# Two moves of TensorE work inside the sixteen steps of a selective scan: the sums over states, the first convolution and the time-step projection

## The chip, the cores and the metric

The kernel runs as one program on one core of one Trainium2 chip. The metric is the device time of one execution in microseconds (us). Everything is fp32. A measurement of this kernel tells changes of about 0.2% from none.

## What is computed

The program is four layers one after the other on x of shape (2, 128, 64, 64). The change touches layer 0 only, a four-way selective scan (Mamba): the 4096 tokens of each of the 2 images are normalised over the 128 channels and scanned in four directions (row by row and column by column, each forwards and backwards), and the four outputs go through one fusing projection and are added to x. One direction is, cut to what matters:

```python
xz = x @ W_in.T
xh, z = jnp.split(xz, 2, axis=-1)              # 256 inner channels each
xh = silu(causal_conv4(xh) + conv_b)
x_dbl = xh @ W_xp.T                            # 8 for dt, 16 for B, 16 for C
dt = softplus(x_dbl[..., :8] @ W_dt.T + b_dt)
dA  = exp(dt[..., None] * A)                   # A: 256 channels x 16 states
dBu = dt[..., None] * Bm[:, :, None, :] * xh[..., None]
h_t = dA_t * h_{t-1} + dBu_t                   # scan over tokens
y = einsum('lbdn,bln->bld', hs, Cm) + xh * Dp  # sum over the 16 states
out = (y * silu(z)) @ W_out.T
```

Layers 1 and 2 are attention over 4096 positions, layer 3 is a second, small Mamba with a group norm. They are the same before and after.

## The kernel before, in words

**Chunks and steps.** Layer 0 is cut into 64 chunks of T = 512 tokens: image, then row or column order, then forwards or backwards, then 8 chunks (`chunks`). Chunks 0-7, 16-23, 32-39 and 48-55 run forwards, the others backwards. A chunk has 16 steps (`for s in range(16)`), one per unit u of 128 x 1024 elements: 128 partitions hold 4 states x 32 channels, and the free axis holds 2 blocks of 512 tokens. The order of all instructions is written out by hand under `tc.manual_schedule()`; each engine works off its own instructions in that order. Three chunks are in flight: `c` is scanned, `new` (the next) has its time step and B, C prepared, `nxt` (the one after) has its convolution made. `old` is the chunk before.

**One step s**, in the order of the source:

- `s_dbu` (L330, POOL): dBu of unit s+2. `dbu` has three buffers, so it waits for the scan of unit s-1.
- `s_scan` (L374, DVE): the scan of unit s.
- `V[s]`: extra DVE work, `dt_` (L306) in steps 5 and 6, the norm's `mul` (L194) in step 8 and `sub` (L161) in step 13.
- `s_hc` (L386 on DVE, or L384 on POOL for units 0, 5, 9, 11, 14): h times C for unit s-1. `hc` has four buffers.
- `s_da` (L343, ACT): dA of unit s+1 into one of two PSUM buffers, so it waits for the scan of unit s-1; `s_fix` (L358, ACT): adds the carried state to the first token of dBu of unit s+1. The scan of unit s+1 waits for it. The first chunk of a direction has no `s_fix`.
- `s_hst` (L379, ACT), then the list `A[s]` of extra ACT work.
- on TensorE (PE): `y0` (L390) in steps 3 and 11, the sums over states `s_y` (L397), then `M[s]`, then `s_pc` (L363), which spreads C over the partitions for `s_hc` two units at a time.
- `yg_(1)` of the old chunk at the end of step 1 and `yg_(0)` at the end of step 10 (L404, DVE): y times the gate.

**The sums over states.** `s_y(u)` is two matmuls of 128*32 by 128x512; a pair of units is 4 matmuls, 8 passes in the records. `pairs` says in which step a pair is issued: units 0,1 in step 3; 2,3 in 5; 4,5 in 8; 6,7 in 9; 8,9 in 12; 10,11 in 14; 12,13 in 15; 14,15 in step 1 of the next chunk. Units 0-7 add into one `y` tile and 8-15 into the next; `y` has one buffer. So `yg_(0)` waits for the sum of units 6,7 and `yg_(1)` for that of 14,15.

**The tile `misc`.** All other PSUM results of layer 0 share one PSUM buffer, `misc`: each user is a matmul in `M[s]` and a reader on ACT or DVE, and the next matmul into `misc` waits for that reader. In order: step 15 `pd` (L267), step 0 reader `xd_` (L272); `pt(0)` (L287, the time step's projection), reader `abs_(0)` (L294) in step 1; `pt(1)` in step 1, readers `abs_(1)` and then `e_exp` (L297) in step 2; `po` (L415, L419) in step 2, reader `xo` in step 4; `pt` again in steps 4 and 5 for `dt_`; `pz(0)` (L241) in step 6 with reader `z_` (L247); the norm's `scale` (L191) in step 7; `px(0)`, the first convolution (L228, four matmuls, 8 passes), in step 8 with its reader `x_(0)` (L237) in step 9; `px(1)` in step 10 with `x_(1)` in step 12; the norm's `center` (L157) in step 12; `pz(1)` in step 13; the norm's `var` (L170) in step 14. `e_ln` (L300, with a table load ahead of it and one after it) is in step 3.

**Norms and turns.** The normalisation of later tokens is mixed into chunks 0-3 and 15-22, its second half (`lp`: `rows`, `scale`, `mul`, `affine` L197) into the chunk after each. Chunks 6-13 and 32-39 have one copy more on ACT in step 11, which turns the picture. Below, "norm chunks" are chunks 1-4 and 16-22, which hold a second half of a norm (and all but chunk 4 a first half too); "plain forward" chunks are the other forward ones that are not first in their direction, 18 in number; "backward" chunks that are not first number 28.

Of the kernel before, what the change touches and what calls it, by code (L numbers as in the profile page):

```python
# [56 lines left out]
def conv_seq_kernel(ctx: ExitStack, tc: tile.TileContext, a: dict, out: bass.AP):  # L57
# [36 lines left out]
    with ExitStack() as c0:  # L94
# [104 lines left out]
        def turn(j):  # L199

            nc.scalar.copy(
                xnt[:, 3 + j * T : 3 + (j + 1) * T].rearrange("p (w h) -> p w h", h=H),
                xn[:, 3 : L + 3].rearrange("p (h w) -> p w h", w=W)[:, 8 * j : 8 * j + 8, :],
            )
# [234 lines left out]
        pairs = {}  # L439
# [3 lines left out]
        with tc.manual_schedule():  # L443
            c, c1 = chunks[:2]
# [110 lines left out]
            old = None  # L555
            for k, c in enumerate(chunks):
                new, nxt = (chunks[k + i] if k + i < nk else None for i in (1, 2))
                ln, lp = norms.get(k), norms.get(k - 1)

                def at(u):  # L560
                    return (c, u) if 0 <= u < 16 else ((old, u + 16) if u < 0 else (new, u - 16))

                A, V, M, G = {}, {}, {}, {}
                if old is not None:
                    M[2], A[4] = old.po, (old.xo,)
                if c.rev:
                    A[4] = (*A[4], c.zload)
                else:  # L570
                    A[8] = (c.zsilu,)
                if new is not None:
                    A[0] = (new.xd_,)
                    M[0], A[1] = lambda: new.pt(0), (lambda: new.abs_(0),)
                    M[1], A[2] = lambda: new.pt(1), (lambda: new.abs_(1), new.e_exp)
                    A[3] = (new.e_ln,)
                    M[4], V[5] = lambda: new.pt(0), lambda: new.dt_(0)
                    M[5], V[6] = lambda: new.pt(1), lambda: new.dt_(1)
                    G[7], G[8] = lambda: new.dtu_(0), lambda: new.dtu_(1)
                    if not new.rev:  # L580
                        M[6], A[7] = lambda: new.pz(0), (lambda: new.z_(0),)
                        M[13], A[14] = lambda: new.pz(1), (lambda: new.z_(1),)
                if nxt is not None:
                    M[8], A[9] = lambda: nxt.px(0), (lambda: nxt.x_(0),)
                    M[10], A[12] = lambda: nxt.px(1), (lambda: nxt.x_(1),)
                    A[13] = (nxt.xsilu,)
                    M[15] = nxt.pd
                if lp is not None:
                    A[3] = (*A[3], lp.ln, lp.exp)
                    A[6] = (lp.rows,)  # L590
                    M[7], V[8] = lp.scale, lp.mul
                    A[10] = (lp.affine,)
                if ln is not None:
                    M[12], V[13] = ln.center, ln.sub
                    A[14] = (*A.get(14, ()), ln.square)
                    M[14], A[15] = ln.var, (ln.keep,)
                if k in turns:
                    A[11] = (lambda: turn(turns[k]),)

                for s in range(16):  # L600
                    (c1, u1), (c2, u2), (cp, up) = at(s + 1), at(s + 2), at(s - 1)

                    if c2 is not None:
                        c2.s_dbu(u2)
                    c.s_scan(s)
                    if s in V:
                        V[s]()
                    if cp is not None:
                        cp.s_hc(up)
                    if s in G:  # L610
                        G[s]()

                    if c1 is not None:
                        c1.s_da(u1)
                        c1.s_fix(u1)
                    if cp is not None:
                        cp.s_hst(up)
                    for f in A.get(s, ()):
                        f()

                    if s in (3, 11):
                        c.y0(s // 11)
                    for cy, e in ((c, s), (old, s + 16)):
                        for u in pairs.get(e, ()) if cy is not None else ():
                            cy.s_y(u)
                            cy.s_y(u + 1)
                    if s in M:
                        M[s]()
                    if s % 2 and s < 15:
                        c.s_pc(s + 1)  # L630
                    elif s == 15 and new is not None:
                        new.s_pc(0)

                    if s == 1 and old is not None:
                        old.yg_(1)
                    if s == 10:
                        c.yg_(0)

                    if new is not None:
                        if s in (7, 14):  # L640
                            new.spread("dts", s // 14)
                        if s in (9, 13):
                            new.spread("dus", s // 13)
                        if s in (8, 10, 12, 14):
                            new.states(0, s // 2 - 4)
                        if s in (11, 12, 13, 15):
                            new.states(1, GROUPS_C[{11: 0, 12: 1, 13: 2, 15: 3}[s]])
                old = c
# [20 lines left out]
    with ExitStack() as c1:  # L669
# [296 lines left out]
        for n, j in enumerate(jobs):  # L966
# [10 lines left out]
            if jobs[n - 1].layer == 1:  # L977
                for ci in range(NCH):
                    c = Conv(jobs[n - 1].b, ci)
# [3 lines left out]
        with tc.manual_schedule():  # L983
# [13 lines left out]
            for slot in range((len(groups) + 2) * UPG):  # L997
                u = slot % UPG
                G = at(slot)[0]
                if G is not None:  # L1000
                    G.score(u)
                    nxt = at(slot + UPG)[0]
                    if u == 10 and nxt is not None:
                        nxt.q = nxt.job.query(nxt.g)
                G, d = at(slot - 1)
                if G is not None:
                    G.larger(d)
                G = at(slot - UPG)[0]
# [7 lines left out]
                G, d = at(slot - UPG - 5)  # L1016
                if G is not None and d % 2 == 0:
                    G.prob(d // 2)
                G, d = at(slot - UPG - 6)
                if G is not None and d % 2 == 0:  # L1020
                    G.expo(d // 2)
                G, d = at(slot - UPG - 8)
                if G is not None:
                    G.value(d)
                G, d = at(slot - UPG - 7)
                if G is not None and d % 2 == 0 and d:
                    G.total(d // 2)
                G, d = at(slot - 2 * UPG)
# [13 lines left out]
    with ExitStack() as c3:  # L1042
# [269 lines left out]
        V, G = nc.vector, nc.gpsimd  # L1312
# [6 lines left out]
        with tc.manual_schedule():  # L1319
            c = chunks[0]  # L1320
# [13 lines left out]
            for s in range(-1, len(steps) + 3):  # L1334
# [3 lines left out]
                old = chunks[ci - 1] if ci > 0 else None  # L1338
# [209 lines left out]
```

## Time and profile before

| what | value |
|---|---|
| three runs | 6811.3, 6818.59, 6804.39 us; median 6811.3 |
| the profiled execution | 6810.44 us, span 6808.7 us (1.7 us outside the span) |
| granted TensorE clock, mean | 0.857 |
| layer 0, first scan to end of the last | 57.15 to 3474.5 us of the span: 3417.35 us |
| busy in that stretch | PE 2898.43, DVE 3271.78, ACT 2749.80, POOL 3271.53 us |
| layers 1-3 | 3474.5 to 6808.7 us |
| one norm chunk (chunk 18) | 1028.11 to 1084.86: 56.75 us; DVE 52.37, POOL 51.30, ACT 48.23 busy |
| one plain forward chunk (chunk 53) | 2897.67 to 2951.37: 53.70 us; DVE 51.31, POOL 51.59, ACT 45.76 |
| one backward chunk (chunk 30) | 1686.60 to 1739.70: 53.10 us; DVE 51.08, POOL 50.99, ACT 41.39 |

How to read it: a chunk starts where its first scan (L374) starts, so every sixteenth L374 record of the trace is a chunk's start, and the distance between two scans is the length of a step. A timeline line has the start in us from the span's start, the length in us, engine, line, operation, tiles and count; in brackets stands how long the engine sat idle just before and what it is taken to have waited for. Consecutive records of the same kind are merged in it, with their number after "x".

### The profile page before, as it was taken

To read this page: it belongs to the slowest core of one execution; us is meant where nothing else is said; L and a number is where in the kernel's file an instruction comes from. 1 tells how busy PE (TensorE), PEld (TensorE's weight loads), DVE (VectorE), ACT (ScalarE), POOL (GpSimd) and SP (SyncE) were. 2 spreads that over 40 slices of the span, in tenths; PEclk is the share of its full clock that TensorE was granted. 3 is DMA by queue.
4 is the path that set the end of the run, shared out by engine and by line. 5 is a ranking of instruction groups with operands and counts; after the bars stand their busy time and mean duration, and the time that the engine had idled before them with its cause. 6 is when DMAs were issued, how large, how long until landed. Compare 5 with 4: busy or idle time off the path is not lost. (4 is left out here: it accounts for less than half of the span.)

```text
span 6808.7 us, 67303 instructions
## 1 busy us (share of the span) xinstructions
PE 6005.6 (88%) x20652; PEld 2821.7 (41%) x20652; DVE 5524.3 (81%) x4499; ACT 4461.8 (66%) x7666; POOL 5362.4 (79%) x2487
## 2 busy tenths in 40 slices
PE   8888888888888888888879999999999997888888
PEld 2222222222222222222238887787788884222222
DVE  7999999999999999999966665565566675787777
ACT  7887778877788777887745664555456564434342
POOL 6899998899999999999956664555566666777776
PEclk7777777777778777777779999999999998988888
DMA  6565655566566656665630000000000001222221
GB/s 170 138 149 145 157 145 140 137 154 150 141 159 152 157 143 154 150 154 146 148 93 2 4 4 1 1 1 1 1 1 13 1 1 61 75 71 72 90 75 67
DMA packets 352652, 616.51 MB, mean 91 GB/s; under 512 B 72473, under 2 KB 74786, under 8 KB 351650
## 3 DMA queue, kind: packets, MB, share of 16 engines
q1 hardware_dynamic: 351552, 610.44, 35.2%
q8 instruction: 162, 2.65, 0.2%
q14 instruction: 200, 1.64, 0.1%
q10 hardware_dynamic: 738, 1.78, 0.1%
HBM read 496.45 MB, written 115.47 MB: 90 GB/s over the span
## 5 line engine op out<-in xcount | busy, mean ns | idle before, releaser
L330 POOL TENSOR_TENSOR dbu<-dus,bs 128x1024 f32<-128x1024 f32 x1024 | 2404.0, 2374 | 157.0 <-DVE h L374 141.1
L374 DVE TENSOR_TENSOR_SCAN h<-da,hst,dbu 128x1024 f32<-128x1024 f32 x896 | 2094.3, 2345 | 77.8 <-ACT dbu L358 75.0
L343 ACT ACTIVATE da<-dts,aneg 128x512 f32<-128x512 f32 (+1 forms) x2048 | 1412.6, 690 | 443.7 <-DVE h L374 404.1
L890 POOL TENSOR_TENSOR sum<-sum,sc 128x1024 f32<-128x1024 f32 x384 | 906.8, 2362 | 496.7 <-ACT sc L885 493.1
L852 ACT COPY sc<-s 128x512 f32<-128x512 f32 x1024 | 598.1, 585 | 867.7 <-PE s L847 753.5
L859 DVE TENSOR_TENSOR mx<-mx,s 128x512 f32<-128x512 f32 x896 | 610.1, 681 | 569.5 <-ACT sc L852 568.5
L847 PE MATMUL s<-q,k 128*128 128x256 f32 x4096 | 1058.0, 382 | 11.7 <-ACT q L833 8.4
L902 PE MATMUL av<-sc,v 128*128 128x256 f32 x4096 | 1049.6, 379 | 2.3 <-ACT sc L885 2.3
L397 PE MATMUL y<-hc,cst 128*32 128x512 f32 x4096 | 811.3, 760 | 179.2 <-DVE hc L386 103.8
L386 DVE TENSOR_TENSOR hc<-h,pc 128x1024 f32<-128x1024 f32 x704 | 844.9, 1200 | 0.1
L847 PEld LDWEIGHTS s<-q,k 128*128 128x128 f32 x4096 | 781.2, 192 | 146.2 <-issue 36.6
L902 PEld LDWEIGHTS av<-sc,v 128*128 128x128 f32 x4096 | 769.1, 190 | 103.1 <-ACT sc L885 3.7
L384 POOL TENSOR_TENSOR hc<-h,cs 128x1024 f32<-128x1024 f32 x320 | 758.2, 2369 | 1.3 <-issue 1.3
L363 PE MATMUL pc<-xd,sel 16*128 16x512 f32 x1024 | 713.4, 788 | 4.8 <-DVE hc L386 4.1
L1217 POOL TENSOR_TENSOR A<-A,D 128x1024 f32<-128x1024 f32 x224 | 525.9, 2365 | 225.2 <-DVE D L1222 200.3
L882 DVE TENSOR_TENSOR sc<-sc,pm 128x1024 f32<-128x1024 f32 x512 | 620.9, 1214 | 0.9 <-PE pm L878 0.9
L885 ACT ACTIVATE sc<-sc 128x1024 f32<-128x1024 f32 x512 | 542.3, 1059 | 8.6 <-DVE sc L882 8.1
L287 PE MATMUL misc<-xd,w_dt 9*128 9x512 f32 x504 | 386.5, 855 | 155.1 <-ACT x L426 83.6
L1210 ACT ACTIVATE A<-dtr,aneg 128x1024 f32<-128x1024 f32 (+1 forms) x256 | 246.0, 1032 | 380.8 <-PE y L1242 363.0
L397 PEld LDWEIGHTS y<-hc,cst 128*32 128x32 f32 x4096 | 104.9, 117 | 745.6 <-issue 337.4
L1228 DVE TENSOR_TENSOR A<-A,q 128x1024 f32<-128x1024 f32 (+1 forms) x256 | 276.9, 1082 | 148.4 <-PE q L1194 148.2
L1194 PE MATMUL q<-xs,lb 32*128 32x512 f32 x896 | 331.5, 712 | 72.0 <-DVE D L1204 65.7
(263 smaller groups left out, 8078.4 us busy)
## 6 DMA issues: line engine op xcount, KB each, us to landing
dts<-ddt SPq DMA_DIRECT2D x512, 256.0 KB, 5.5
dus<-ddu SPq DMA_DIRECT2D x512, 256.0 KB, 5.1
bs<-rows SPq DMA_DIRECT2D x1024, 64.0 KB, 4.9
cs<-rows SPq DMA_DIRECT2D x1024, 64.0 KB, 3.3
ddt<-dt SPq DMA_DIRECT2D x128, 256.0 KB, 2.0
ddu<-dtu SPq DMA_DIRECT2D x128, 256.0 KB, 4.1
dtr<-ddt SPq DMA_DIRECT2D x448, 64.0 KB, 1.9
rx<-ddx SPq DMA_DIRECT2D x448, 64.0 KB, 1.9
```

What stands on the lines that cost most here:

```text
L330: nc.gpsimd.tensor_mul(t, self.dus[q], _bc(self.bs[g], 1, [P, 2, T]))
L343: act(t[:, i, sl], self.dts[q][:, i, sl], AF.Exp, scale=an[:, g, 2 * q + i : 2 * q + i + 1])
L363: mm(t, lhsT=sel[32:48, 4 * g : 4 * g + 4, :].rearrange("p n d -> p (n d)"), rhs=self.xd[32:48, :], start=True, stop=True)
L374: nc.vector.tensor_tensor_scan(ho, ai, bi, init, ALU.mult, ALU.add)
L384: nc.gpsimd.tensor_mul(t, self.h[u], _bc(self.cs[gq(u)[0]], 1, [P, 2, T]))
L386: nc.vector.tensor_mul(t, self.h[u], _bc(self.pc[u // 2], 1, [P, 2, T]))
L397: mm(self.y[q // 2][r : r + 32, :], lhsT=sum4, rhs=self.hc[u][:, i, :], start=False, stop=(u % 8 >= 6), skip_group_check=True)
L847: mm(p[:, o, :], lhsT=j.k[m // 8][:, m % 8 * P : m % 8 * P + P], rhs=self.q, start=True, stop=True)
L859: nc.vector.tensor_max(self.mx, self.s[0][:, 0:2, :] if u == 1 else self.mx, self.p[u])
L882: nc.vector.tensor_sub(s, s, _bc(self.pm[:, :], 1, [P, 4, NQ]))
L890: nc.gpsimd.tensor_add(self.sum, self.s[0] if w == 1 else self.sum, self.s[w])
L902: mm(self.av, lhsT=self.job.v[m // 8][:, m % 8, :], rhs=self.s[u // 2][:, m % 4, :], start=(m == 0), stop=(m == 31))
```

## The change

No instruction is added or taken away. On PE, in every chunk, two things change places with a sum over states:

- `px(0)` of `nxt` goes from the end of step 8 to the end of step 9, behind the sum of units 6,7; its reader `x_(0)` on ACT goes from step 9 to step 10, and there behind the norm's `affine`.
- `pt(0)` of `new` goes from the end of step 0 to step 1, behind the sum of units 14,15 of the chunk before. Its reader `abs_(0)` stays where it was, in step 1.

The source lines of `y0` and `s_y` are put ahead of `s_da` to make that order; as those run on other engines, their orders don't change by it. The order of PE around the two places:

```
before:  pd  pc(0)  pt(0)  s_y(14,15)  pt(1)  pc(2)  po ...
after:   pd  pc(0)  s_y(14,15)  pt(0)  pt(1)  pc(2)  po ...

before:  pc(8)  s_y(4,5)  px(0)  s_y(6,7)  pc(10)  px(1)  y0(1)  pc(12)  s_y(8,9)
after:   pc(8)  s_y(4,5)  s_y(6,7)  px(0)  pc(10)  px(1)  y0(1)  pc(12)  s_y(8,9)
```

The orders of DVE, POOL and of the DMA queue (SP) are the same in both. ACT's differs only in the place of `x_(0)`.

```diff
-                A, V, M, G = {}, {}, {}, {}
+                A, V, F, M, G = {}, {}, {}, {}, {}
...
                 if new is not None:
                     A[0] = (new.xd_,)
-                    M[0], A[1] = lambda: new.pt(0), (lambda: new.abs_(0),)
+                    F[1], A[1] = lambda: new.pt(0), (lambda: new.abs_(0),)
                     M[1], A[2] = lambda: new.pt(1), (lambda: new.abs_(1), new.e_exp)
...
                 if nxt is not None:
-                    M[8], A[9] = lambda: nxt.px(0), (lambda: nxt.x_(0),)
+                    M[9], A[10] = lambda: nxt.px(0), (lambda: nxt.x_(0),)
                     M[10], A[12] = lambda: nxt.px(1), (lambda: nxt.x_(1),)
...
-                    A[10] = (lp.affine,)
+                    A[10] = (lp.affine, *A.get(10, ()))
...
+                    if s in (3, 11):
+                        c.y0(s // 11)
+                    for cy, e in ((c, s), (old, s + 16)):
+                        for u in pairs.get(e, ()) if cy is not None else ():
+                            cy.s_y(u)
+                            cy.s_y(u + 1)
+                    if s in F:
+                        F[s]()
+
                     if c1 is not None:
                         c1.s_da(u1)
                         c1.s_fix(u1)
...
-                    if s in (3, 11):
-                        c.y0(s // 11)
-                    for cy, e in ((c, s), (old, s + 16)):
-                        for u in pairs.get(e, ()) if cy is not None else ():
-                            cy.s_y(u)
-                            cy.s_y(u + 1)
                     if s in M:
                         M[s]()
```

## The prediction

> **What bounds the kernel now.** I read first the windows by stage. Layer 0 (57.15 to 3474.50 us) is the only stage that the change touches: in its 3417 us DVE is busy 3272 and POOL 3272, each 96%, so at most 3417 - 3272 = 145 us can be won, and any wait put on DVE is lost at once. Next the waits of DVE between 200 and 3400 us (us in total, times, longest):
>
> ```profile
> DVE h L374 <- ACT dbu L358: 73.2, 126, 1.4
> DVE dt L404 <- PE y L397: 35.8, 33, 2.4
> DVE dt L404 <- issue: 19.3, 10, 2.9
> DVE dt L306 <- PE misc L287: 5.2, 8, 0.8
> ```
>
> Two things: the gate L404 waits for the sums over states (35.8 + 19.3 = 55.1 us, which the change is about), and the scan L374 waits for ACT's `s_fix` L358 (73.2 us), which it leaves. Then the timeline of a norm chunk, 18, steps 8 to 13:
>
> ```profile
> 1058.98 1.94 PE L397 MATMUL y<-hc,cst 128*32 128x512 f32 x8
> ...
> 1060.84 5.46 PE L228 MATMUL misc<-xnt,wk 128*128 128x512 f32 x8
> ...
> 1066.23 1.07 PE L397 MATMUL y<-hc,cst 128*32 128x512 f32 x8
> 1066.34 0.69 ACT L237 ACTIVATE xs<-misc,vec 128x512 f32<-128x512 f32 x1 [3.83 <-PE misc L228]
> ...
> 1067.42 0.69 DVE L404 TENSOR_TENSOR dt<-sz,y 128x512 f32<-128x512 f32 x1 [2.28 <-PE y L397]
> ...
> 1068.68 2.35 DVE L374 TENSOR_TENSOR_SCAN h<-da,hst,dbu 128x1024 f32<-128x1024 f32 x1 [0.57 <-ACT dbu L358]
> ...
> 1074.81 1.12 PE L157 MATMUL misc<-x,meanw 128*128 128x512 f32 x2
> ...
> 1076.56 0.66 DVE L161 TENSOR_TENSOR xc<-x,misc 128x512 f32<-128x512 f32 x1
> ```
>
> The sum of units 6,7 (1066.23) stands behind the convolution (1060.84), and the gate and the next scan wait 2.28 + 0.57 us. PE has no gap from 1058.98 to 1075.93, the end of `center`; that is the line to keep in mind. Last, the timeline of a plain forward chunk, 53, steps 0 to 5:
>
> ```profile
> 2897.53 1.12 PE L363 MATMUL pc<-xd,sel 16*128 16x512 f32 x2
> ...
> 2900.45 1.78 PE L287 MATMUL misc<-xd,w_dt 9*128 9x512 f32 x2 [1.80 <-ACT xd L272]
> ...
> 2902.16 1.94 PE L397 MATMUL y<-hc,cst 128*32 128x512 f32 x8
> ...
> 2902.27 0.60 ACT L294 ACTIVATE e<-misc 128x512 f32<-128x512 f32 x1 [0.18 <-PE misc L287]
> 2903.42 1.42 ACT L343 ACTIVATE da<-dts,aneg 128x512 f32<-128x512 f32 x2 [0.56 <-DVE h L374]
> ...
> 2906.14 0.60 ACT L294 ACTIVATE e<-misc 128x512 f32<-128x512 f32 x1 [0.90 <-PE pc L363]
> 2906.76 1.06 ACT L297 ACTIVATE e<-e 128x1024 f32<-128x1024 f32 x1
> ...
> 2914.54 0.37 ACT L358 ACTIVATE dbu<-hst,dbu,df 128x1 f32<-128x1 f32 x1
> ...
> 2914.95 2.35 DVE L374 TENSOR_TENSOR_SCAN h<-da,hst,dbu 128x1024 f32<-128x1024 f32 x1
> ```
>
> From `abs_(1)` (2906.14) ACT runs nearly without a gap (exp, dA, table load, ln, table load, dA) to `s_fix` of unit 5 (2914.54), and scan 5 starts 0.04 us after it. The same distance, 0.03 to 0.09 us, stands in 44 of the 45 plain forward and backward chunks that I went through, 0.2 us in most norm chunks: scan 5 is set by ACT, and ACT's run by `abs_(1)`.
>
> **What the Trainium skill says.** "TensorE: Matmul & The Clock Gate", Part 2: TensorE pulls weight loads ahead, but its matmuls stay in program order. So a sum that waits for `hc` holds up `pt(0)` or `px(0)` behind it; the trace has the mirror case above. The same page, Part 1: the clock is at half rate unless the engine was busy in a window of about 3.4 us. The trace agrees in kind: a pair of sums takes 1.07 or 1.94 us, `pt(0)` 1.12 or 2.07. "ScalarE: Activation LUTs", What ACT_TABLE_LOAD costs: about 1283 ns; the trace has 1.28 (L300, L343), so ACT's run can't shrink.
>
> **The change, part by part.** No instruction comes or goes. Durations are of the profiled execution (6810.4 us, span 6808.7), which lies 0.9 us under the median of 6811.3; I add to the median.
>
> *Step 1, `pt(0)` behind the sum of 14,15, plain forward.* The sum waits for `hc` of unit 15, which ends at 2901.13 (2899.93 + 1.20). At the low clock, which PE already has there (1.94): sum to 2903.05, `pt(0)` to 2905.05, `abs_(0)` to 2905.7. Behind `abs_(0)` on ACT stand dA of unit 3 (was 2903.42, now 2905.7), `s_fix`, `s_hst` and `abs_(1)`; behind it on PE `pt(1)`, now 2905.75 to 2907.8. So `abs_(1)` starts at 2907.85 instead of 2906.14: +1.7 us, and all of it reaches scan 5. What the gate wins in step 1 (0.77 us here) is lost, for DVE then waits for the same `s_fix`. At the high clock (1.07, 1.12, 1.12) `abs_(1)` would not move: 0. With each chunk's own old durations the mean over 18 chunks is 1.3, with all at the low clock 2.2. I take 1.7: 18 x 1.7 = 31 us (bounds 3 and 40).
>
> *The same, backward.* Here `s_fix` of unit 4 often waits for POOL's dBu of unit 4 (mean end 11.57 us after the chunk's start, dA of unit 4 ends at 10.95), which covers 0.6 us of delay; means over 27 chunks 0.4 (old durations), 1.6 (low clock), 0 (high). If POOL's cover were gone, 0.75. *Step 9, backward:* `hc` of unit 7 ends 31.5 us into the chunk, while `px(0)` used to run from 27.2 to 32.2. Now: sum to 33.4, `px(0)` (5.0) to 38.4, `x_(0)` to 39.1, dA of unit 12 to 40.5 and its `s_fix` to 40.9, against scan 12 at 41.0: just covered. `px(1)` ends at 43.2 (was 38.0), `x_(1)` starts 43.2 (was 41.75), so dA of unit 14 starts at 43.9 instead of 43.4: +0.5 at scan 15, where scan waits for ACT already. The sum of 8,9 ends at 46.2, and DVE's `hc` of unit 12 wants its buffer at 45.6: +0.6, the same half microsecond. POOL, always busy from unit 8 to the next chunk's unit 4, takes part of both. I take 0.6 in all: 28 x 0.6 = 17 us (bounds -3, if the gate's 0.3 us were won and nothing lost, and 45).
>
> *Step 9, plain forward:* `px(0)` starts 2.7 us later, DVE has 0.6 us or more of slack at scan 12 and the sum of 8,9 just makes it: 0. Where a turn stands on ACT in step 11 (14 chunks) I add 0.2: 3 us.
>
> *Norm chunks.* The sum of 6,7 goes to 1060.9, the gate to scan 10's end (1065.14) and scan 11 to 1065.8: 2.28 + 0.57 = 2.85 us won. But PE's gapless row has the same work in it, so `center` still ends at 1075.93, or up to 0.87 us later if the sum now runs at 1.94 instead of 1.07. DVE would reach L161 at 1073.8 and waits there until 1076.0 to 1076.9: of 2.85 are left +0.56 to -0.3. ACT, no longer held 3.83 us by `x_(0)`, has its work of steps 13 to 15 done earlier, which can win the 0.75 us that scan 0 waits in the next chunk. Against it stands step 1 with +0.9 (old durations; the clock is high there), less if `pd` comes earlier. I take -0.8: 11 x -0.8 = -9 us (bounds -2.8 x 11 = -31 and +7).
>
> First chunks of a direction have no `s_fix` and slack: 0. Layers 1 to 3: unchanged. DVE, POOL and SP are in the old order; the DMAs of `rows` hang on `xd_`, which is not moved. Sum: 31 + 17 + 3 - 9 = 42; I give 6850.
>
> **The rivals.**
> - *Faster: the sums bind and nothing takes their place.* For it: 55 us of waits at L404, nearly all in norm chunks. It needs PE at its high clock when the sum of 14,15 runs (1.07 and 1.12, when `abs_(1)` doesn't move) and `center` not the next wait. Then the 11 norm chunks win 2.85 us each: 6811 - 31 = 6780. It decides from the point where the plain chunks lose under 31/46 = 0.7 us each. Against it: in chunk 53 PE is at 1.94 at exactly that place, and the gapless row before `center`.
> - *Same: POOL is the true bound.* POOL has 51.0 to 51.6 us of work in a chunk of 53.1 to 53.7, and a delay of DVE that POOL outlasts costs nothing. Then the forward chunks lose about 0.9 (16), the backward none, the norm chunks win 1.4 (15): 6812. Against it: POOL itself waits 134 us for scans in the 3200 us window.
> - *Much slower:* low clock in all chunks, and backward chunks without cover: 40 + 45 + 3 + 7 = 95: 6906.
>
> **How the numbers follow.** Forecast 6850, its own range 6826 to 6890: chance 0.52. Faster rival 0.27, same 0.14, much slower 0.07. The range of 8 in 10 reaches down into the faster rival, 6778, and up to 6900: out are half of the faster case and part of the slowest, under 2 in 10. The bounds of 0.2% (what a measurement of this kernel can tell from no change) are 6798 and 6825: faster 0.27, same 0.14, slower 0.59.
>
> **What would show it.** The order is fixed by hand, so that the change is in effect is seen in the trace by L397 ahead of L228 in step 9. Right: L404 <- PE y falls from 55 us to under 15; DVE h L374 <- ACT L358 grows from 73 to over 100, at scan 5 of forward chunks; L161 in norm chunks waits for L157. Plain forward chunks grow by 1 to 2 us, norm chunks hardly shrink. Wrong: `abs_(1)` in forward chunks where it was (PE at the high clock), or norm chunks of 55 us or less.

## The result, and the profile after

Five runs of the changed kernel have a median of 6881.27 us (6868.47 to 6885.65), five of the kernel before 6811.3 us (6797.26 to 6818.59). The ratio is 1.0101, with a 95% interval of 1.0084 to 1.0118: slower by 1%. The profiled execution took 6885.65 us (span 6883.9), 75.2 more than the profiled one of before, with a mean clock of 0.859.

Cut at every sixteenth L374 as before, the 75.2 us lie here (each kind's sum is that of its chunks' lengths, after less before):

| chunks | mean before, us | mean after, us | sum, us | predicted, us |
|---|---|---|---|---|
| 18 plain forward | 52.99 | 53.53 | +9.7 | +31 and +3 |
| 28 backward, 15 among them | 52.84 | 54.31 | +41.3 | +17 |
| 11 norm | 57.33 | 57.50 | +1.8 | -9 |
| 7 first of a direction | 50.48 | 52.76 | +16.0 | 0 |
| layer 0 in all | | | +68.8 | +42 |
| layers 1-3 and the ends | | | +6.4 | 0 |

The windows by stage first (length of the stretch, then busy us of PE, PEld, DVE, ACT and POOL with the number of instructions, then clock, DMA share and GB/s):

```profile
57.40:3543.30 3485.90, 2952.98 (x7758) 803.87 (x7758) 3278.09 (x2004) 2737.54 (x5231) 3269.76 (x1469) 0.77 0.59 145
```

DVE and POOL have the same work as before (3278 and 3270 us against 3272 and 3272) in a stretch that is 68 us longer. So the loss is waiting: the work of these two engines became no dearer. What DVE waits for, between 200 and 3400 us of the span (us in total, times, longest):

```profile
DVE h L374 <- ACT dbu L358: 126.5, 155, 2.0
DVE xc L161 <- PE misc L157: 14.6, 9, 1.6
DVE hc L386 <- PE y L397: 14.2, 29, 0.9
DVE dt L404 <- PE y L397: 12.6, 10, 1.5
DVE h L374 <- POOL dbu L330: 7.8, 6, 1.8
```

The wait that the change aims at, L404 for the sums, fell from 55.1 to 12.6 us. But the scans' wait for ACT grew from 73.2 to 126.5, and L161 and L386 are new in the list. Now the three kinds of chunk, each by the timeline. Norm chunk 18 (its first scan at 1050.01), steps 8 to 13:

```profile
1083.06 3.64 PE L397 MATMUL y<-hc,cst 128*32 128x512 f32 x16
...
1086.64 4.70 PE L228 MATMUL misc<-xnt,wk 128*128 128x512 f32 x8
...
1089.14 0.67 DVE L404 TENSOR_TENSOR dt<-sz,y 128x512 f32<-128x512 f32 x1
...
1098.86 1.13 PE L157 MATMUL misc<-x,meanw 128*128 128x512 f32 x2
...
1100.02 0.69 DVE L161 TENSOR_TENSOR xc<-x,misc 128x512 f32<-128x512 f32 x1 [1.65 <-PE misc L157]
```

The sums of units 4 to 7 are one run now, and L404 has no wait in brackets. The wait is at L161 instead, for `center`: 1.65 us. Plain forward chunk 53 (first scan at 2954.61), steps 1 to 5:

```profile
2959.11 1.12 PE L287 MATMUL misc<-xd,w_dt 9*128 9x512 f32 x2
...
2960.26 0.60 ACT L294 ACTIVATE e<-misc 128x512 f32<-128x512 f32 x1 [1.23 <-PE misc L287]
...
2960.91 0.69 PE L287 MATMUL misc<-xd,w_dt 9*128 9x512 f32 x1 [0.69 <-ACT e L294]
...
2961.45 0.59 PE L287 MATMUL misc<-xd,w_dt 9*128 9x512 f32 x1
...
2962.47 0.58 ACT L294 ACTIVATE e<-misc 128x512 f32<-128x512 f32 x1
...
2971.38 2.35 DVE L374 TENSOR_TENSOR_SCAN h<-da,hst,dbu 128x1024 f32<-128x1024 f32 x1 [0.35 <-ACT dbu L358]
```

`pt(0)` takes 1.12 us here and `pt(1)` 1.13 (passes of 0.69 and 0.59, which overlap): TensorE is at its high clock. `abs_(1)` starts 7.86 us into the chunk, and before it was 8.47. This chunk got shorter. Of backward chunk 45, first its second convolution and the scan of unit 15 in the kernel before (first scan at 2474.60):

```profile
2508.56 3.70 PE L228 MATMUL misc<-xn,wk 128*128 128x512 f32 x8
...
2515.88 0.68 ACT L237 ACTIVATE xs<-misc,vec 128x512 f32<-128x512 f32 x1
...
2524.85 4.59 DVE L374 TENSOR_TENSOR_SCAN h<-da,hst,dbu 128x1024 f32<-128x1024 f32 x2 [0.64 <-ACT dbu L358]
```

The convolution's reader `x_(1)` (2515.88) comes when its turn on ACT comes, 3.6 us after the result is there. The same chunk after (first scan at 2526.20), steps 9 to 15:

```profile
2558.90 1.92 PE L397 MATMUL y<-hc,cst 128*32 128x512 f32 x4 [1.45 <-DVE hc L386]
...
2560.75 4.92 PE L228 MATMUL misc<-xn,wk 128*128 128x512 f32 x8
...
2565.72 0.69 ACT L237 ACTIVATE xs<-misc,vec 128x512 f32<-128x512 f32 x1 [2.77 <-PE misc L228]
...
2566.66 3.70 PE L228 MATMUL misc<-xn,wk 128*128 128x512 f32 x8
...
2570.20 1.02 PE L390 MATMUL y<-xs,diag_d 128*128 128x512 f32 x2
...
2571.26 0.69 ACT L237 ACTIVATE xs<-misc,vec 128x512 f32<-128x512 f32 x1 [1.45 <-PE y L390]
2571.84 1.41 ACT L343 ACTIVATE da<-dts,aneg 128x511 f32<-128x511 f32 x2
...
2573.30 1.22 DVE L386 TENSOR_TENSOR hc<-h,pc 128x1024 f32<-128x1024 f32 x1 [0.36 <-PE y L397]
...
2579.16 4.59 DVE L374 TENSOR_TENSOR_SCAN h<-da,hst,dbu 128x1024 f32<-128x1024 f32 x2 [1.26 <-ACT dbu L358]
```

Read it from the bottom: scan 15 (2579.16) waits 1.26 us for ACT; ACT was late with dA of unit 14 (2571.84), since that stands behind `x_(1)` (2571.26). And `x_(1)` did not wait for `px(1)` (ended 2570.36), but started 0.04 us after the end of `y0(1)` (2571.22). The last part of this matters below. The same kernel and chunk, steps 1 and 2:

```profile
2529.68 1.92 PE L397 MATMUL y<-hc,cst 128*32 128x512 f32 x4 [1.89 <-DVE hc L386]
...
2531.53 2.07 PE L287 MATMUL misc<-xd,w_dt 9*128 9x512 f32 x2
...
2533.64 0.60 ACT L294 ACTIVATE e<-misc 128x512 f32<-128x512 f32 x1 [2.85 <-PE misc L287]
...
2534.29 1.21 PE L287 MATMUL misc<-xd,w_dt 9*128 9x512 f32 x1 [0.69 <-ACT e L294]
...
2536.40 0.60 ACT L294 ACTIVATE e<-misc 128x512 f32<-128x512 f32 x1 [0.46 <-PE pc L363]
```

TensorE stands idle for 1.89 us until `hc` of unit 15 is there, and then works at about half its rate: 1.92 us for a sum that takes 1.05 in chunk 53, 2.07 for `pt(0)`. `abs_(1)` starts 10.20 us into the chunk; before it was 7.45. (In the chunks beside it, after, it is 8.39 and 10.20 in turn; means over all 9.40 and 7.94.) In the same place of the kernel before, this line shows what stood in for ACT:

```profile
2486.09 0.39 ACT L358 ACTIVATE dbu<-hst,dbu,df 128x1 f32<-128x1 f32 x1 [1.07 <-POOL dbu L330]
```

There `s_fix` of unit 4 waits 1.07 us for POOL. After the change it no longer does: POOL's dBu of unit 4 ends 10.21 us into a backward chunk in the mean instead of 11.56.

### The profile page after: what moved, and what is told of

Its sections match the earlier page's. It is cut to its first block, busy times and chain, and to the rows that moved or that the text cites. A ratio compares the mean times of both kernels' runs of the same rounds, so it can differ in the third digit from the quotient of the medians.

```text
span 6883.9 us, 67303 instructions
## 1 busy us (share of the span) xinstructions
PE 6060.5 (88%) x20652; PEld 2826.2 (41%) x20652; DVE 5536.3 (80%) x4499; ACT 4447.8 (65%) x7666; POOL 5358.7 (78%) x2487
## 3 DMA queue, kind: packets, MB, share of 16 engines
q8 instruction: 162, 2.65, 0.2%
## 5 line engine op out<-in xcount | busy, mean ns | idle before, releaser
L374 DVE TENSOR_TENSOR_SCAN h<-da,hst,dbu 128x1024 f32<-128x1024 f32 x896 | 2093.5, 2343 | 139.3 <-ACT dbu L358 133.8
L397 PE MATMUL y<-hc,cst 128*32 128x512 f32 x4096 | 908.5, 762 | 260.9 <-DVE hc L386 230.8
L386 DVE TENSOR_TENSOR hc<-h,pc 128x1024 f32<-128x1024 f32 x704 | 844.3, 1199 | 19.3 <-PE y L397 14.6
L885 DVE TENSOR_TENSOR sc<-sc,pm 128x1024 f32<-128x1024 f32 x512 | 620.9, 1213 | 0.9 <-PE pm L881 0.9
L397 PEld LDWEIGHTS y<-hc,cst 128*32 128x32 f32 x4096 | 126.1, 120 | 933.1 <-DVE hc L386 481.1
```

Of the source, the lines that this page charges most:

```text
L374: nc.vector.tensor_tensor_scan(ho, ai, bi, init, ALU.mult, ALU.add)
L386: nc.vector.tensor_mul(t, self.h[u], _bc(self.pc[u // 2], 1, [P, 2, T]))
L397: mm(self.y[q // 2][r : r + 32, :], lhsT=sum4, rhs=self.hc[u][:, i, :], start=False, stop=(u % 8 >= 6), skip_group_check=True)
L885: nc.vector.tensor_sub(s, s, _bc(self.pm[:, :], 1, [P, 4, NQ]))
```

## The experiments

Each of the twelve was timed beside the kernel before, and its ratio is to those runs. Lengths of chunks are means from each one's profile, to be held against the table above: norm means chunks 1-4 and 17-22 (57.42 before, 57.84 after), backward leaves out 15 (52.84, 54.32), first backward is 8, 24, 40 and 56 (50.05, 53.55). A profile is one execution, and lies up to 17 us off the median of its kernel's runs. The chunks that hold a second half of a norm are twelve: the eleven norm chunks and chunk 23, which the table has among the plain forward ones.

### Which of the two moves, and where

The changed kernel with `pt(0)` back in step 0, so that only the convolution moves:

```diff
-                    F[1], A[1] = lambda: new.pt(0), (lambda: new.abs_(0),)
+                    M[0], A[1] = lambda: new.pt(0), (lambda: new.abs_(0),)
```

> Only the convolution moves behind the sum of units 6,7 (the time step's projection stays in step 0). Theory (both moves delay ACT, and POOL's work covers part of either): backward chunks +0.6 us each by scan 15 waiting for ACT behind the later x_(1), first backward chunks +1.6, norm chunks about -1, plain forward 0: about 12 us over the kernel before, 6823. Rival 1 (the losses of the two moves simply add up to the 69 us of layer 0): about +34, 6845. Rival 2 (step 1 does all the harm and step 9 is the gain it was meant to be): norm chunks -2.5 us each, 6785 or less.

Measured: 6824.56 us, ratio 1.0019 (1.0007 to 1.0030). The norm chunks fall to 54.77, a gain of 26.5 us; the backward chunks grow to 53.83 (+26.8) and the first backward ones by 11.5 in sum; plain forward +0.5. So the move in step 9 does what it is for in norm chunks, and pays it back in backward ones. The time of the theory (6823) came true, but its parts did not: -1 was said for a norm chunk and +0.6 for a backward one. And POOL's dBu of unit 4 ends 10.09 us into a backward chunk here, by this move alone.

The other half, with the convolution back in step 8, so that only `pt(0)` moves:

```diff
-                    M[9], A[10] = lambda: nxt.px(0), (lambda: nxt.x_(0),)
+                    M[8], A[9] = lambda: nxt.px(0), (lambda: nxt.x_(0),)
```

> Only the time step's projection moves behind the sum of units 14,15 (the convolution stays in step 8). Theory: abs_(1) and with it scan 5 come later; plain forward +0.5 us a chunk, backward +0.4, first backward +2.4, norm +0.5: about +35, 6846. Rival 1 (losses add): also about +35, so that the sum with the other part tells: 47 or 69. Rival 2 (all harm is in step 1): +90, 6900.

Measured: 6822.93 us, ratio 1.0025 (1.0013 to 1.0036), about half of the loss expected; norm chunks +5.9 us in sum, plain forward -3.1, backward +0.1, first backward +7.1, first forward +4.9. In backward chunks POOL's dBu of unit 4 still ends 11.56 us after the start, as before, and covers the delay of ACT. The two halves cost 11.6 and 13.5 us of layer 0, together 25; the whole change costs 68.8. Each half makes the other dearer.

The kernel before, with the convolution moved only in chunks that hold a second half of a norm:

```diff
-                    M[8], A[9] = lambda: nxt.px(0), (lambda: nxt.x_(0),)
+                    if lp is not None:
+                        M[9], A[10] = lambda: nxt.px(0), (lambda: nxt.x_(0),)
+                    else:
+                        M[8], A[9] = lambda: nxt.px(0), (lambda: nxt.x_(0),)
...
-                    A[10] = (lp.affine,)
+                    A[10] = (lp.affine, *A.get(10, ()))
```

> The convolution moves behind the sum of units 6,7 only in the 12 chunks that hold a second half of a norm; nothing else moves. Theory: PE's gapless row holds up center, so the gate's wait of 2.3 us comes back as a wait of about 1.6 us at the norm's subtraction in step 13; the chunks win about 1 us each: 6811 - 12 = 6799. Rival (nothing takes the place of the gate's wait): 11 x 2.85 = 31 us, 6780.

Measured: 6781.44 us, ratio 0.9953 (0.9940 to 0.9965), faster than both kernels, and the rival's time, not the theory's. The norm chunks are 54.77 again (-26.5 us), every other kind is within 3 us in sum of where it was. Its norm chunk 18 (first scan at 1015.41), to be read beside that of the changed kernel:

```profile
1046.85 3.27 PE L397 MATMUL y<-hc,cst 128*32 128x512 f32 x16
...
1050.05 3.70 PE L228 MATMUL misc<-xnt,wk 128*128 128x512 f32 x8
...
1062.43 0.69 DVE L161 TENSOR_TENSOR xc<-x,misc 128x512 f32<-128x512 f32 x1 [0.96 <-PE misc L157]
```

The convolution takes 3.70 us here and 4.70 there, and L161 waits 0.96 instead of 1.65.

### Where the gain of the norm chunks went

First, whether `center` is the next wait of these chunks. The kernel above, with `center` also ahead of the sum of 8,9 in step 12:

```diff
-                    M[12], V[13] = ln.center, ln.sub
+                    (F if lp is not None else M)[12], V[13] = ln.center, ln.sub
...
+                    if s in F:
+                        F[s]()
                     for cy, e in ((c, s), (old, s + 16)):
```

> As the run before, and in those chunks the norm's center is put on PE ahead of the sum of units 8,9 instead of behind it. Theory: center ends about 1 us earlier, the wait at the subtraction falls from 1.6 to about 0.5 us, and norm chunks win about 2 us each: 6811 - 23 = 6788. Rival (ACT, not center, sets the norm chunks): same time as the run before within 5 us.

Measured: 6796.56 us, ratio 0.9970 (0.9958 to 0.9982). That is 15 us slower than without this move, though the two intervals overlap. The theory missed: norm chunks became longer in the profile, 56.30 instead of 54.77. In chunk after chunk the convolution alternates between 3.7 and 4.7 us. In chunks 3, 20 and 22, where it is at 3.7, the wait at L161 is nearly gone (0.04 us), and they still take 56.0 us. So the position of `center` is not what carries these chunks, and the length of the convolution, which is the clock, moved without anything of it having been changed.

Then both moves, in norm chunks only (the changed kernel's order there, that of before elsewhere):

```diff
-                    M[0], A[1] = lambda: new.pt(0), (lambda: new.abs_(0),)
+                    if lp is not None:
+                        F[1] = lambda: new.pt(0)
+                    else:
+                        M[0] = lambda: new.pt(0)
+                    A[1] = (lambda: new.abs_(0),)
```

> Both moves, but only in the 12 chunks that hold a second half of a norm. Theory (the two moves hinder each other there: the later scan 5 of step 1 throws the chunk out of the state with TensorE at its high clock during the convolution, so that it falls back from 54.6 to about 58 us): norm chunks 57.5 to 58 us, the whole about 6811. Rival (the step 1 move costs what it costs alone, 0.6 us a chunk): norm chunks 55.4 us, the whole about 6788.

Measured: 6807.54 us, ratio 1.0008 (1.0000 to 1.0017), norm chunks 57.79, as the theory said. The second move in these chunks, `pt(0)` behind the sum of 14,15, loses 3.0 us of each, all that the first had won. `abs_(1)` comes 1.9 us later and scan 5 1.7; but the convolution is also at 4.70 us again and the sum of 6,7 at 1.94.

Which of the two is it, ACT's delay in step 1 or the clock in step 9? Zero passes tell them apart: two matmuls of a tile of zeros, 4 passes, added into `y`, which leave its values as they are and keep TensorE busy.

```diff
+        zw = gt([P, P], "zw", wp)
+        nc.vector.memset(zw, 0.0)
...
+            def warm(self, i):
+                for _ in range(2):
+                    mm(self.y[i], lhsT=zw, rhs=cst[:, 0:T], start=False, stop=False,
+                       skip_group_check=True)
...
+                    M[3] = lambda: c.warm(0)
```

The last line stands in chunks with a second half of a norm only. In the kernel with the convolution alone moved there (ratio 0.9953 without zeros):

> The convolution behind the sum of 6,7 only in the 12 chunks with a second half of a norm (the fastest so far), and in those chunks four passes of matmuls by zeros in step 3, behind the sum of 0,1, so that TensorE has less idle time ahead of the convolution. Theory (norm chunks are set by TensorE's clock): sums of 4,5 run at 1.07 too and a norm chunk falls from 54.6 to about 53.5: 6770. Rival (54.6 is set by ACT and DVE, the clock is no longer the limit): same as without the zeros, 6781, or a little slower by the added passes.

Measured: 6774.11 us, ratio 0.9954 (0.9943 to 0.9966), norm chunks 54.70 (54.77 without). The rival holds: where the convolution is already at 3.70 us, the zeros bring nothing and cost nothing. In the kernel with both moves there (1.0008 without):

> Both moves only in the 12 chunks with a second half of a norm, with the same added passes by zeros in step 3 of those chunks. Theory (there, too, the low clock during the sum of 6,7 and the convolution carries the loss): the convolution takes 3.7 us again instead of 4.7, norm chunks fall from 57.8 to 55.5 or less, the whole to about 6788. Rival (the order of the two moves itself makes the 57.8 us): 6807 or more.

Measured: 6805.75 us, ratio 1.0006 (0.9998 to 1.0015), norm chunks 57.82. This one missed its aim, as the timeline of TensorE in its chunk 18 shows (lines shifted: L243 is `pz`, L230 the convolution):

```profile
1056.17 2.08 PE L243 MATMUL misc<-xnt,m 128*128 128x512 f32 x2 [2.75 <-DVE dt L308]
...
1066.50 4.70 PE L230 MATMUL misc<-xnt,wk 128*128 128x512 f32 x8
```

Behind the zeros of step 3 TensorE stood idle for 2.75 us ahead of `pz(0)`, and `pz(0)` took 2.08 us, the rate of the low clock; the convolution is at 4.70 us as without the zeros. Nothing follows from it on the rival. So zeros in that gap as well, in both kernels:

```diff
+                    M[5] = lambda: (new.pt(1), c.warm(0))
```

> Both moves only in the 12 chunks with a second half of a norm, with four passes by zeros in step 3 and four more in step 5 behind pt(1), into the 2.75 us in which TensorE sat idle ahead of pz(0) in the run before. Theory (the low clock from pz(0) to the middle of the convolution carries the loss in norm chunks): the sums of 4,5 and 6,7 take 1.07 us, the convolution 3.7, norm chunks fall from 57.8 us to 55 or less: 6780 or less. Rival (the order of the two moves itself makes the 57.8 us): 6805 or more, with the convolution at 3.7 us all the same.

Measured: 6772.29 us, ratio 0.9957 (0.9944 to 0.9970), norm chunks 54.77. Its chunk 18 (first scan at 1016.48, L230 the convolution, L404 the sums, L163 `sub`):

```profile
1047.60 3.31 PE L404 MATMUL y<-hc,cst 128*32 128x512 f32 x16
...
1050.84 3.70 PE L230 MATMUL misc<-xnt,wk 128*128 128x512 f32 x8
...
1063.22 0.69 DVE L163 TENSOR_TENSOR xc<-x,misc 128x512 f32<-128x512 f32 x1 [0.41 <-PE misc L159]
```

Both moves are in it, and yet it is as fast as the kernel without the second. The sums are not at the 1.07 us a pair that was expected (3.31 for two pairs), but the convolution is at 3.70. The 3.0 us between 57.79 and 54.77 are the zeros' work alone, in two places. The stretch from scan 5 to scan 14, with the sums and the convolution in it, is 2.1 us shorter (30.14 instead of 32.24). And scan 5 comes 1.1 us earlier (18.21 instead of 19.27), because TensorE is faster where one chunk passes into the next. There stand the norm's `var` and the sum of units 12,13; ahead of chunk 18 first without zeros (L170, L397; first scan at 1029.23) and then with them (L172, L404):

```profile
1027.25 1.87 PE L170 MATMUL misc<-meanw,sq 128*128 128x1 f32 x8 [2.00 <-ACT sq L165]
1029.04 1.93 PE L397 MATMUL y<-hc,cst 128*32 128x512 f32 x8
```

```profile
1014.49 1.05 PE L172 MATMUL misc<-meanw,sq 128*128 128x1 f32 x8 [2.02 <-ACT sq L167]
1015.47 1.16 PE L404 MATMUL y<-hc,cst 128*32 128x512 f32 x8
```

The same zeros in the kernel with the convolution alone moved:

> The convolution behind the sum of 6,7 only in those 12 chunks, with the same added passes by zeros in steps 3 and 5. Theory (clock): norm chunks fall from 54.7 us to 53.5 or less: 6768 or less. Rival (ACT and DVE set 54.7): 6775 to 6785.

Measured: 6777.21 us, ratio 0.9959 (0.9945 to 0.9972), norm chunks 55.86 (59.6 and 59.7 in chunks 1 and 2, 54.3 to 55.7 in the others): nothing won where `pt(0)` is in its old place, so that the zeros are no gain in themselves. In norm chunks the clock carries the loss: with `pt(0)` late, TensorE runs at about half its rate where one chunk passes into the next, and again up to the middle of the convolution of step 9. In step 1 itself it doesn't: in chunk 18 the sum of 14,15 and `pt(0)` take 1.06 to 1.07 and 1.12 us, with zeros and without.

### Where backward chunks lose

The changed kernel, with `x_(1)` behind dA of unit 14 where no first half of a norm is in the chunk:

```diff
-                    M[10], A[12] = lambda: nxt.px(1), (lambda: nxt.x_(1),)
-                    A[13] = (nxt.xsilu,)
+                    M[10] = lambda: nxt.px(1)
+                    if ln is not None:
+                        A[12], A[13] = (lambda: nxt.x_(1),), (nxt.xsilu,)
+                    else:
+                        A[13] = (lambda: nxt.x_(1), nxt.xsilu)
```

> The changed kernel, with the reader of the second convolution, x_(1), put behind dA of unit 14 on ACT (step 13 instead of 12) in chunks without a first half of a norm. Theory: in backward chunks dA of unit 14 waits behind x_(1), which waits for the convolution that step 9 made late; with x_(1) behind it, dA of unit 14 starts at scan 12's end again and backward chunks get back 0.6 us or more of their 1.5: about 20 us under the changed kernel, 6860. Rival (the buffer of hc for unit 12, which waits for the late sum of 8,9, is the limit): scan 15 stays where it was in the changed kernel, within 5 us of 6880.

Measured: 6861.39 us, ratio 1.0083 (1.0071 to 1.0096). dA of unit 14 starts at 43.91 instead of 45.02 and scan 15 at 51.82 instead of 52.33; backward chunks are 53.85 instead of 54.32 (-12.7 us in sum), the first backward ones 51.61. Plain forward chunks lose most of it again, 54.13 instead of 53.53. So `x_(1)` in front of dA is a good part of the backward loss, as taking it from there gives back 0.47 us of 1.48, but not the whole of it.

Why `x_(1)` is late was still open. It starts 0.90 us after `px(1)`'s end and 0.04 us after `y0(1)`'s, in each of 25 backward chunks, and in the same way when the convolution alone is moved. `xs` has two buffers for three chunks in flight, so `x_(1)` of the chunk after next writes where `y0(1)` of the scanned chunk reads. A third buffer wasn't tried. Instead `y0(1)` reads another tile, so that half of the term `xh * Dp` comes from another chunk's tokens:

```diff
-            def y0(self, i):
+            def y0(self, i, d=None):
...
-                mm(self.y[i], lhsT=diag_d[:, i, :], rhs=self.xs[i], start=True,
+                mm(self.y[i], lhsT=diag_d[:, i, :], rhs=(d or self).xs[i], start=True,
...
-                        c.y0(s // 11)
+                        c.y0(s // 11, new if s == 11 else None)
```

> The changed kernel, with one operand changed: y0(1) of the scanned chunk reads xs[1] of the next chunk instead of its own, so that the term xh * Dp of the upper 128 inner channels is made from the wrong chunk's tokens (the last chunk keeps its own). No instruction comes, goes or moves. In the changed kernel x_(1) starts 0.04 us after the end of y0(1) in all 25 backward chunks looked at, and 0.90 us after the end of px(1); xs has two buffers for three chunks in flight, so x_(1) writes where y0(1) has just read. Theory (x_(1) waits for y0(1) to free the buffer, and this is the half microsecond that the prediction missed in step 9): x_(1) starts within 0.1 us of px(1)'s end, 0.8 to 0.9 earlier (43.5 us into a backward chunk instead of 44.41), dA of unit 14 at 44.1 to 44.3 instead of 45.02, scan 15 about 0.5 earlier, backward chunks 53.8 to 54.0 instead of 54.32 (as with x_(1) put behind dA of unit 14, 53.85), plain forward chunks within 0.2 of 53.53; 6861 to 6872. Rival 1 (x_(1) waits for something else on TensorE): x_(1) stays 0.9 behind px(1), nothing changes, 6875 to 6888. Rival 2 (the buffer wait is real but the hc buffer of unit 12 and the sum of 8,9 bind as well): x_(1) earlier by 0.9, scan 15 where it was, backward chunks 54.2 or more, 6875 to 6888.

Measured: 6837.4 us (6 runs, 6828.63 to 6847.44), ratio 1.0049 (1.0034 to 1.0064). Its backward chunk 45 (first scan at 2495.39), steps 11 to 15:

```profile
2536.11 3.70 PE L228 MATMUL misc<-xn,wk 128*128 128x512 f32 x8
...
2539.65 1.02 PE L390 MATMUL y<-xs,diag_d 128*128 128x512 f32 x2
...
2539.85 0.69 ACT L237 ACTIVATE xs<-misc,vec 128x512 f32<-128x512 f32 x1 [0.59 <-PE misc L228]
...
2540.43 1.41 ACT L343 ACTIVATE da<-dts,aneg 128x511 f32<-128x511 f32 x2
...
2547.75 2.35 DVE L374 TENSOR_TENSOR_SCAN h<-da,hst,dbu 128x1024 f32<-128x1024 f32 x1 [0.41 <-ACT dbu L358]
```

`x_(1)` starts 0.04 us after `px(1)`'s end (2539.81) while `y0(1)` is running, and scan 15 waits 0.41 instead of 1.26. In the mean over these chunks `x_(1)` is at 43.50 (44.41 with its own tile), dA of unit 14 at 44.19 (45.02), scan 15 at 51.50 (52.33): the theory's mechanism is shown. Its size was put too low. Backward chunks came to 53.54, 0.78 less instead of 0.5, the first backward ones to 50.91 (-10.6 us in sum) and the norm chunks to 56.63 (-12.1), with forward ones a little longer (53.82). Rival 2 falls with it: the `hc` of unit 12 waits for its buffer as before (14.0 us, 29 times), and it doesn't bind. In norm chunks the wait for `y0(1)` is there before the change too (`x_(1)` 0.90 us behind `px(1)`'s end); taking it away together with the move in these chunks alone wasn't tried.

What is left is the clock, and this was tried the other way round, with the changed kernel untouched but for zeros in step 0 (ahead of the sum of 14,15) and, where no second half of a norm is in the chunk, in step 8:

```diff
+                if lp is None:
+                    M[8] = lambda: c.warm(0)
...
+                    M[0] = lambda: old.warm(1)
```

> The changed kernel with four passes of matmuls by a block of zeros added on TensorE in each chunk's step 0 (ahead of the sum of 14,15) and, except in chunks with a second half of a norm, in step 8 (between the sums of 4,5 and 6,7), where TensorE sits idle; they add zero to y. Theory (the low TensorE clock behind the idle time carries the loss): sums and projections there take 1.07 and 1.12 us instead of 1.94 and 2.07, abs_(1) and x_(1) come earlier, backward chunks get back over half of their 1.5 us: 6850 or less. Rival (order and waiting alone carry it): no better than the changed kernel, 6880 or more.

Measured: 6833.66 us, ratio 1.0042 (1.0030 to 1.0054), mean clock 0.886 instead of 0.859. Backward chunks are 52.95, 0.11 more than before the change, first backward ones 50.30. Backward chunk 45 (first scan at 2502.27; L230 is the convolution, L392 `y0`, L239 `x_`, L376 the scan):

```profile
2534.72 3.70 PE L230 MATMUL misc<-xn,wk 128*128 128x512 f32 x8
...
2539.40 3.70 PE L230 MATMUL misc<-xn,wk 128*128 128x512 f32 x8
...
2543.99 0.69 ACT L239 ACTIVATE xs<-misc,vec 128x512 f32<-128x512 f32 x1
...
2552.88 4.59 DVE L376 TENSOR_TENSOR_SCAN h<-da,hst,dbu 128x1024 f32<-128x1024 f32 x2 [0.63 <-ACT dbu L360]
```

The first convolution takes 3.70 us instead of 4.92, `x_(1)` comes at 41.9 instead of 44.4, and scan 15 waits 0.63 us for ACT, as in the kernel before (0.64). At the high clock the new order costs the backward chunks next to nothing, waits for `y0(1)` included. So the two causes can't be added: taking away the wait alone gives back 0.78 of the 1.48 us, taking away the low clock alone 1.37. Of the 33.5 us that layer 0 still loses in this profile (an execution 17 us above the median), most lie elsewhere: plain forward 9.4, norm chunks with 15 and 16 12.9, first forward ones 7.3. What sets those was not taken further.

## Why the prediction was right, and where its sum was off

The direction, the time within its range and the mechanism were right: the sums' wait goes, and what was behind the moved matmuls on ACT comes late. For the 42 us forecast in layer 0, 68.8 came, and the parts differ more than the sum. That the sum came this near is in part luck: plain forward chunks were put 24 us too high and backward ones 24 us too low, which cancel.

- *The gate is relieved, the scans wait for ACT, L161 waits for `center`.* Right: 55.1 to 12.6, 73.2 to 126.5, and L161 with 14.6 us in 9 waits, up to 1.65 each.
- *Step 1, plain forward, +1.7 each, 31 us.* The term was mis-sized: +0.54 each, 9.7 us. The path through `abs_(1)` to scan 5 holds (scan 5 starts 0.58 later in the mean, the chunk is 0.54 longer), but I took TensorE to be at the low clock there because chunk 53 was before. After, `pt(1)` takes 1.13 us in that chunk and not the 2.05 of the prediction, and so it goes in half of these chunks. The nine in which `pt(1)` takes 2.07 us became 1.28 us longer in the mean; the nine in which it takes 1.12 became 0.21 shorter, where the prediction had 0 for the high clock. So the price was right for each rate, and what was wrong is how many chunks run at the low one. Step 1 alone cost these chunks nothing (-3.1 in sum), so the clock of before was no property of the place. (The +3 for turns beside it counts five backward chunks among its 14.)
- *Step 9, backward, +0.5.* This step failed, by what it left out. With the convolution alone moved, the stations that it gave came true to 0.2 us: sum to 33.25 (33.4 said), `px(0)` to 38.31 (38.4), `px(1)` to 43.00 (43.2). But `x_(1)` started at 43.89 and not with the end of `px(1)`, because it overwrites what `y0(1)` reads. I had followed the reader to its queue, not to the buffer that it writes. Scan 15 came 1.07 later, the chunk 0.99. With this wait taken away, dA of unit 14 is, after allowing for step 1 (scan 5 0.48 later), at 43.7: +0.3 of the +0.5 forecast.
- *Step 1, backward, nearly covered by POOL.* True for step 1 alone (+0.1 us in 27 chunks), false for both. The move in step 9 makes the end of a chunk later for DVE; POOL runs ahead, and its dBu of unit 4 ends 10.21 us into the chunk instead of 11.56 (10.09 with the move in step 9 alone, 11.56 with that in step 1 alone). `pd` and `pc(0)` come earlier too (`pc(0)` starts 0.54 us ahead of the chunk instead of 1.71 behind its start), TensorE stands idle ahead of the sum, and `pt(1)` takes 2.07 us in the mean instead of 1.61. So scan 5 is 0.6 later, the chunk another 0.49. The prediction named the price without POOL's cover (0.75) but didn't see that its own step 9 takes the cover away.
- *`hc` of unit 12, +0.6 at the same half microsecond.* The wait came (14.2 us, 29 times, 0.4 in a backward chunk) and cost nothing that was seen: it stayed when `x_(1)` was early, and the scan was earlier all the same.
- *Norm chunks, -0.8 each.* -9 was said, +1.8 came. That little is left was right, and the reason given, the gapless row ahead of `center`, was half of it: with the convolution alone moved, 2.65 us of 2.85 are won, though `center` comes no earlier in the order. What lost the gain was step 1, by 3.0 us and not 0.9, through the clock between two chunks (1.1 us) and between scan 5 and scan 14 (2.1 us). The Trainium skill, "TensorE: Matmul & The Clock Gate", Part 1, says that the window by which the clock is set runs freely, so that the turn depends on where in it the work falls. The runs agree as far as they go: the same eight passes of the convolution, some 2 us later in the chunk, take 4.70 us instead of 3.70.
- *First chunks, 0.* +16.0, of which 14.0 in the four first backward ones. They have no `s_fix`, but dA stands behind the same `abs_(1)` and `x_(1)`; with `y0(1)` reading another tile 10.6 of the 14.0 are gone, with zeros 13.0.
- *The rivals.* The faster one had the norm chunks' gain right: 26.5 us were won of 31 said, where only they were changed. Its condition, that the plain chunks lose under 0.7 us each, held for forward (0.54) and not for backward chunks (1.48). That POOL is the true bound falls with the backward chunks' growth.

The +6.4 us in layers 1-3, whose code is the same, are taken for scatter between executions: in the profiles of the twelve experiments, which leave these layers alone as well, this part is from 19.4 us less to 6.7 more than in that of before.

## What to carry to other kernels

Follow a moved matmul three steps: to its reader's place in the reader's queue, to what stands behind the reader there, and to the buffer that the reader writes, with who still reads that buffer. Two moves that each cost little can take away each other's cover, so that costs out of one profile don't add (11.6 and 13.5 us became 68.8): try them apart. And move only where the wait is: the norm chunks held nearly all of it, and one of the two moves, made in the twelve chunks with a second half of a norm alone, won 0.47% (0.35 to 0.60) where the whole change lost 1%.

## What the runs showed of the hardware

More work on TensorE made kernels faster: 8 passes of zeros in each norm chunk (1.0008 without, 0.9957 with them), and 4 to 8 in each chunk of the changed kernel (1.0101 without, 1.0042 with). A gap of 2.75 us was enough for the clock to be found low behind it, and so was a shorter one. In the kernel with the convolution moved in norm chunks alone, TensorE has one gap between 1133.69 and 1145.20, of 1.40 us, in its chunk 20 (first scan at 1124.89). The next matmuls are at the high rate, `pt(0)` with 1.12 us. But from `pt(1)` on they are at the low one, with no further gap: its first pass takes 1.22 us, where it took 0.69 in chunk 53 above.

```profile
1143.09 1.12 PE L287 MATMUL misc<-xd,w_dt 9*128 9x512 f32 x2 [1.40 <-ACT x L426]
...
1145.21 1.22 PE L287 MATMUL misc<-xd,w_dt 9*128 9x512 f32 x1
```

Work without a gap doesn't soon bring the high clock back either. In norm chunk 18 of the kernel before, TensorE stands idle for 0.68 us ahead of the norm's `scale`, and then no more until the end of `center`:

```profile
1054.97 2.07 PE L191 MATMUL misc<-sq,ones 128*128 128x512 f32 x2 [0.68 <-ACT sz L247]
```

`pc` follows with 2.07 us, then the sum of 4,5 and the convolution (1058.98 and 1060.84 in the prediction's lines). Of the convolution's eight passes the first four still take 1.02 to 1.22 us, and the last four, from 1064.42 on, 0.59: the low rate lasted 9.4 us of gapless work. The prediction quotes a busy window of about 3.4 us as what brings the high rate; this stretch is nearly three times as long, so for such work the rule doesn't hold as quoted. The matmuls in between use 16 rows (`pc`) or 32 columns (the sums) of the array; whether such work counts for less wasn't tried.

The lengths of norm chunks come in steps. Where neighbours are alike they are 57.99 to 58.03 us (before, after, and with both moves in norm chunks alone) or 54.49 to 54.62 (with the convolution alone moved). In other kernels two chunks alternate, 57.66 and 58.38 (`pt(0)` alone moved), 56.61 and 56.02 (`center` earlier), and in the changed kernel's backward chunks 54.02 and 55.23. The section of the skill named above gives the window as 3413 ns. In such windows, 58.02 us are 17 and 54.61 are 16; the pairs, 116.04, 112.63 and 109.25 us, are 34, 33 and 32 to within 0.03 us. It looks as if the loop, whose own speed depends on the clock, falls into step with the window. That is argued from lengths alone; no run here shows the window itself, and not every loop does it: backward chunks 42 to 46 of the kernel before take 52.51 to 52.56 us each, which is 15.4 windows.
